# Empty edge slots: zeroed in DRAM ahead of the scatters, or masked in SBUF as they are read

## The chip, the cores and the metric

The kernel runs on one core of a Trainium2 chip. The metric is device time in microseconds of one execution; the median of three runs before the change is 2573.27 us (2565.25 to 2579.46). The profile is of one further execution, which took 2575.68 us; the span between its first and last instruction is 2573.9 us.

## The reference, cut to what matters

One launch computes a graph network layer and a mixing layer on the same normalised rows, adds both to the input, and then runs a mixture of experts. The change touches only the edges of the graph network: 50,000 edges between 3,125 nodes of 512 features (128 scalars and 128 vectors of three).

```python
ip1 = jnp.einsum('eum,eum->eu', p1[edge_dst], p1[edge_src]) / 3.0
s0 = jnp.concatenate([pd0, pd0, ip1], axis=-1)
...
w = ssp(edge_attr @ W_f1) @ W_f2 * (ssp(s0 @ W_s1) @ W_s2)
w1, w2, w3, w4 = jnp.split(w, 4, axis=-1)
x0e, x1e = split_irreps(x[edge_src])
sh0, sh1 = (edge_sh[:, 0], edge_sh[:, 1:4])
out0 = w1 * x0e * sh0[:, None] + w4 * (jnp.einsum('eum,em->eu', x1e, sh1) / jnp.sqrt(3.0))
out1 = w2[:, :, None] * x0e[:, :, None] * sh1[:, None, :] + w3[:, :, None] * x1e * sh0[:, None, None]
edge_feat = merge_irreps(out0, out1)
out = jax.ops.segment_sum(edge_feat, edge_dst, num_segments=old_x.shape[0])
```

Every term of an edge is multiplied by one of its four numbers `edge_sh`. An edge whose four numbers are zero adds nothing to any node.

## The kernel before, in words

**Where the edges go.** The edges are sorted by target on the chip. The 3,125 targets are cut into 25 groups of 125, each group into two halves of 63 and 62 (with one row shared). Each half has 8 tiles of 128 slots, 1,024 in all, for some 1,000 edges on average; edges beyond them go to shared late tiles. A tile of the first half and a tile of the second form a pair, two pairs form a quad of 512 slots. There are 200 fixed pairs and 8 late pairs that always run: 208 pairs, 104 quads. Further late pairs stand in a loop that runs only if they are needed; the inputs here do not need it.

**The record.** For each edge the first stage makes a record of 48 floats (192 bytes), of which 40 are used: the four numbers of `edge_sh`, the row numbers of source and target, the place of the target in its half, a zero, and 32 numbers of `edge_attr @ W_f1` after softplus. `recs` in DRAM has room for all slots, quad by quad; a quad is 128 x 4 x 48 floats, 98,304 bytes.

**The first stage** (up to 566 us). The edges come in 14 chunks of 28 tiles. For each chunk an attribute load on the SP queue (`edges_of`, L388) is followed by a product on PE (`spread`, L419), softplus on ACT and DVE, and the record is put together (`begin`, `joined`). Beside that, PE counts targets (L260) and ranks edges (`ranked`, L339 to L343), and DVE works out each edge's slot (`places`, L375). POOL then scatters a tile of records at a time into `recs` by an indirect DMA (`place`, L529), 391 in all. The order of the engines is written out by hand in `turns`; a scatter carries a dependence on a PE instruction, so that POOL gives way to PE. Every scatter waits for the DMAs in `cleared` (L183), which write zeros into some quads at the start; SP, ACT and POOL each issue DMAs, and all of these run on the same DMA engines. In the same stage run the layer norm, the mixing layer (`turn_x`, `keys_of`, L920 on) and the node parts of the graph network (L953 to L1032).

**The edge stage** (606 to 1650 us). Its order is the loop over `s` at L1352. For a quad, SP loads its records (`load`, L1104), DVE masks the empty slots (`clear`, L1109), DVE makes the one-hot rows of targets (`which`, L1142), PE turns them (`over`, L1150), POOL gathers the source and target rows (`fetch`, L1123 and L1127), DVE multiplies them (`products`), PE and ACT make the hidden layers, PE the weights (`weigh`, L1262 and L1263), ACT and DVE multiply those together (L1265, L1266), DVE makes the features (`feats`, L1280 and L1284), and PE sums them by target (`gather_up`, L1304). Each step runs some pairs ahead of the next.

**The mask.** An empty slot's record holds whatever lay in DRAM. `clear` combines all 40 used words bit by bit with a mask of all ones or zero, so an empty slot becomes a record of zeros: its rows are row 0, its four numbers 0. The table of masks is `real_slot`: `fixed_real` (L765) fills the fixed part from the number of edges that each half holds, `over_tiles` (L806) the late part.

Of the kernel before, what the change touches and what calls it, by code (L numbers as in the profile page):

```python
# [8 lines left out]
F32 = mybir.dt.float32  # L9
I32 = mybir.dt.int32  # L10
BF16 = mybir.dt.bfloat16
AF = mybir.ActivationFunctionType
ALU = mybir.AluOpType
# [4 lines left out]
P = 128  # L18
# [3 lines left out]
PER = 8  # L22
# [3 lines left out]
PR = 2  # L26
G = 4
REC = 48
# [8 lines left out]
NOV_MOST = 8  # L37
# [14 lines left out]
def gnn_mix_moe_kernel(ctx: ExitStack, tc: tile.TileContext, a: dict, out: bass.AP):  # L52
# [5 lines left out]
    nc = tc.nc  # L58
# [5 lines left out]
    NG = N // TG  # L64
    assert NG * TG == N and NG == NT and T * P >= EDGES > (T - CT) * P
    NU = 2 * NG
    NFIX = PER * NG
# [8 lines left out]
    def tn(t):  # L76
        return min(P, N - t * P)
# [7 lines left out]
    const = ctx.enter_context(tc.tile_pool(name="const", bufs=1))  # L85
# [16 lines left out]
    nc.vector.memset(half, 0.5)  # L102
    pairs_used = const.tile([P, 1], I32, name="pairs_used")
    pair_tile = const.tile([P, 2, NOV_MOST], I32, name="pair_tile")
    real_slot = const.tile([P, NFIX + NOV_MOST, PR], I32, name="real_slot")


    rows_d = dram.tile([N + 2, HID + 3 * MUL], F32, name="rows_d")
# [4 lines left out]
    recs = dram.tile([NQ * G * P, REC], F32, name="recs")  # L113
# [29 lines left out]
    with ExitStack() as c1:  # L143
# [4 lines left out]
        slot_no = srt.tile([P, NOV], I32, name="slot_no")  # L148
# [22 lines left out]
        for r in range(4):  # L171
# [5 lines left out]

        zero = tmp.tile([P, 3 * P], F32, name="zero")
        nc.vector.memset(zero, 0.0)
        by_quad = recs.rearrange("(q p i) f -> p q (i f)", p=P, i=G)  # L180
        per = PER // PR
        cleared = [
            nc.gpsimd.dma_start(by_quad[:, qs, :], zero[:, : G * REC].unsqueeze(1).to_broadcast([P, n, G * REC]))  # L183
            for qs, n in (
                (slice(per - 1, NFIX // PR, per), NG), (slice(NFIX // PR, (NFIX + NOV_MOST) // PR), NOV_MOST // PR),
            )
        ]
        for part in (slice(0, HID), slice(HID, HID + 3 * MUL)):
            nc.gpsimd.dma_start(rows_d[N:, part], zero[:2, : part.stop - part.start])
# [98 lines left out]
        held = srt.tile([P, NG, 2], F32, name="held")  # L288
# [177 lines left out]
        def load(name, shape, src, pool=w, tag=None):  # L466
            t_ = pool.tile(shape, F32, name=name, tag=tag or name)
            nc.scalar.dma_start(t_, src)
            return t_
# [292 lines left out]
        w1t = c4.enter_context(tc.tile_pool(name="w1t", bufs=1, reuse_waits="tile"))  # L762


        def fixed_real():  # L765

            is_real = w1t.tile([P, NG, PER, 2], F32, name="is_real")
            nc.vector.tensor_tensor(
                is_real, slot_no[:, :PER].unsqueeze(1).unsqueeze(3).to_broadcast([P, NG, PER, 2]),
                held.unsqueeze(2).to_broadcast([P, NG, PER, 2]), op=ALU.is_lt,  # L770
            )
            nc.vector.tensor_single_scalar(
                real_slot[:, :NFIX, :].rearrange("p s k -> p (s k)"),
                is_real.rearrange("p b j k -> p (b j k)"), -1.0, op=ALU.mult,
            )

        is_over = w1t.tile([P, NOV], F32, name="is_over")
        steps = w1t.tile([P, P], F32, name="steps")
        own_of = w1t.tile([P, 4], F32, name="own_of")
# [16 lines left out]
        def over_tiles(k):  # L796

            begun = w1t.tile([P, NOV], F32, name="begun", bufs=2)
            nc.vector.tensor_scalar(begun, pair_no, own_of[:, 2 + k : 3 + k], None, op0=ALU.is_ge)
            nc.vector.tensor_scalar(steps, ones, own_of[:, k : k + 1], None, op0=ALU.mult)  # L800
            ps = psum.tile([P, NOV], F32, name="ps_ov", tag="mm")
            nc.tensor.matmul(ps, steps[:NG, :], begun[:NG, :], start=True, stop=True)
            nc.vector.tensor_tensor(is_over, slot_no, ps, op=ALU.is_lt)
            late = w1t.tile([P, NOV], I32, name="late")
            nc.vector.tensor_single_scalar(late, is_over, -1.0, op=ALU.mult)
            nc.vector.tensor_copy(real_slot[:, NFIX:, k], late[:, :NOV_MOST])  # L806
            nc.sync.dma_start(late_real[k], late)
            ps = psum.tile([P, NOV], F32, name="ps_of", tag="mm")
            nc.tensor.matmul(ps, ones[:NG, :], begun[:NG, :], start=True, stop=True)
            late = w1t.tile([P, NOV], I32, name="late")  # L810
            nc.vector.tensor_scalar(late, ps, -1.0, None, op0=ALU.add)
            nc.vector.tensor_copy(pair_tile[:, k, :], late[:, :NOV_MOST])
            nc.sync.dma_start(late_tile[:, k, :], late[0:1, :])
# [81 lines left out]
        def lengths(c):  # L895
# [8 lines left out]
            0: [(sums_turned, 0)], 1: [(values, 0)], 2: [(values_turned, 0), (sums_turned, 1)],  # L904
            3: [(values_out, 0), (values, 1)], 4: [(values_turned, 1)], 5: [(values_out, 1)],
            6: [(through, w_nn[0][:, 1, :], w_nn[0][:, 0, :], w_o[0])], 7: [(through, w_nn[1][:, 1, :], w_nn[1][:, 0, :], w_o[1])],
            8: [(composed,)], 9: [(fixed_real,), (over_steps,)], 10: [(over_tiles, 0)], 11: [(over_tiles, 1)],
        }
        for c in range(NCH):
            pieces.setdefault(2 * c, []).append((lengths, c))  # L910
# [42 lines left out]
        for c in range(NCH):  # L953
# [23 lines left out]
            for t in tiles_of(c):  # L977
                n = tn(t)
# [16 lines left out]
                for o in range(2):  # L995
# [4 lines left out]
                    for i in range(2):  # L1000
                        b = 2 * o + i
# [76 lines left out]
    with ExitStack() as c2:  # L1078
# [27 lines left out]
        def clear(Q, real):  # L1106

            reci = Q.rec.bitcast(I32)[:, :, :USED]
            nc.vector.tensor_tensor(  # L1109
                reci, reci, real.rearrange("p s k -> p (s k)").unsqueeze(2).to_broadcast([P, G, USED]),  # L1110
                op=ALU.bitwise_and,
            )
# [211 lines left out]
        quads = [Quad() for _ in range(n_pairs // PR)]  # L1324
        pairs = [Pair(Q, j) for Q in quads for j in range(PR)]
        with tc.manual_schedule(engines=steady):
            LEAD = 9

            def due(at):

                q, r = divmod(at, PR)
                return [quads[q]] if r == 0 and 0 <= q < len(quads) else []

            def pair(at):

                return [pairs[at]] if 0 <= at < n_pairs else []

            def late_tiles(at):

                return [pair_tile[0:1, k, at - NFIX : at - NFIX + 1] for k in range(2)]  # L1340

            def kept(at):

                if not 0 <= at < n_pairs:
                    return
                R = pairs[at]
                if at >= NFIX:
                    keep_sums(late_tiles(at), R.ps)
                elif at % PER == PER - 1:
                    nc.scalar.copy(acc[:, at // PER, :], R.ps)  # L1350

            for s in range(-LEAD - 5, n_pairs + 1):  # L1352
                for Q in due(s + LEAD + 5):
                    q = quads.index(Q)
                    loaded = load(Q, recs[q * G * P : (q + 1) * G * P, :])
                    if q == 0:
                        for put in placed:
                            waits_for(loaded, put)
                for R in pair(s + LEAD + 3):
                    at = s + LEAD + 3  # L1360
                    if at >= NFIX and R.j == 1:
                        continue
                    if at >= NFIX:
                        R.own = targets([tile_of(nc.sync, v) for v in late_tiles(at)])
                    elif at % PER == 0:
                        R.own = targets([at // PER] * 2)
                    else:
                        R.own = pairs[at - 1].own
                kept(s - 1)
                for Q in due(s + 2):  # L1370
                    softplus2(Q)
                for R in pair(s + 7):
                    products(R)
                for Q in due(s + LEAD + 1):
                    q = quads.index(Q)
                    clear(Q, real_slot[:, PR * q : PR * (q + 1), :])
                    which(Q)
                for Q in due(s + LEAD):
                    over(Q)
                for R in pair(s + 1):  # L1380
                    weigh(R)
                for Q in due(s + 4):
                    hidden(Q)
                    hidden2(Q)
                for Q in due(s + 3):
                    softplus(Q, table)
                for R in pair(s + LEAD):
                    fetch(R.Q, R.j)
                for R in pair(s + 2):
                    scaled(R, 0)  # L1390
                for Q in due(s + 5):
                    turn(Q)
                    turn2(Q)
                for R in pair(s + 2):
                    scaled(R, 1)
                for R in pair(s):
                    if s >= NFIX or s % PER == 0:
                        sums = ps_a.tile([P, D], F32, name="ps_s")
                    R.ps = sums
                    gather_up(  # L1400
                        R, R.ps, s >= NFIX or s % PER == 0, s >= NFIX or s % PER == PER - 1
                    )
                for R in pair(s + 8):
                    own_rows(R)
                for R in pair(s + 1):
                    feats(R)
# [6 lines left out]
        with tc.If(some > NOV_MOST):  # L1413
            with tc.For_i(NOV_MOST // PR, (some + 1) // PR, 1) as i:
                Q = Quad()
# [34 lines left out]
    with ExitStack() as c3:  # L1450
# [18 lines left out]
        with tc.tile_pool(name="work3", bufs=2) as work:  # L1469
# [10 lines left out]
            with tc.manual_schedule(engines={mybir.EngineType.PE}):  # L1480
                oTs = {0: turned(0)}
                for t in range(NT):
                    n = P
# [101 lines left out]
            held = w.tile([P, NE, NT], F32, name="held")  # L1585
# [353 lines left out]
```

## Time and profile before

| | us |
|---|---|
| median of three runs | 2573.27 |
| lowest, highest | 2565.25, 2579.46 |
| the profiled execution | 2575.68 |
| its span | 2573.9 |
| first and last start of a scatter (L529) | 46.2, 564.2 |
| first and last start of a mask (L1109) | 568.6, 1641.4 |
| one mask, median | 0.317 |
| busy over the span: PE, DVE, ACT, POOL | 2347.7, 1634.8, 1254.0, 1529.1 |

A row of the timeline gives start and length in us, the engine, the line of the kernel, the operation with its tiles, and in square brackets how long the engine stood idle before it and what ended that. A name with a q (SPq, POOLq) is the engine's own issue of a DMA or a wait. A row of busy time by stretch gives for each engine its busy us and number of instructions, then the granted clock of TensorE (1.00 is full), the mean busy share of the 16 DMA engines, and GB/s. In the DMA view a queue's row gives packets, MB, and the time that its packets took as a share of 16 engines; q0 is POOL's queue, q1 SP's, q10 ACT's.

### The profile page before, as it was taken

What the parts mean: (1) busy time and instruction counts of PE and PEld (TensorE: products, weight loads), DVE (VectorE), ACT (ScalarE), POOL (GpSimd) and SP (SyncE); (2) the same over time, 40 slices, a digit from 0 to 9 for tenths busy, and PEclk for the clock granted to TensorE, in tenths of its full rate; (3) what the DMA queues carried; (4) which work ended last, traced back from release to release, by engine and by line L of the source; (5) the groups of instructions that cost most, each with busy time, mean ns of one, the idle gap of its engine ahead of it and who ended that gap; (6) DMA issues with size and microseconds to landing.
All of it is one profiled execution on the core that took longest, in us unless ns stands there. A gap on an engine that the chain in (4) does not pass through costs nothing. (4 is left out here: it accounts for less than half of the span.)

```text
span 2573.9 us, 46654 instructions
## 1 busy us (share of the span) xinstructions
PE 2347.7 (91%) x16977; PEld 1522.1 (59%) x16977; DVE 1634.8 (64%) x3130; ACT 1254.0 (49%) x3444; POOL 1529.1 (59%) x1488
## 2 busy tenths in 40 slices
PE   6888999408999999999999999984999999999998
PEld 4654456304444444444444444463888888888887
DVE  8887444207999999999999999976222222222222
ACT  2665512105777777777777777752222222222221
POOL 3777767776666666666666666413555555555552
PEclk7999999758999999999999999997999999999999
DMA  4665889528777777777777777545315325857454
GB/s 145 189 209 198 303 294 312 191 65 262 231 229 232 229 230 228 231 229 231 230 228 227 233 228 231 175 164 209 107 51 183 131 56 192 332 186 258 140 171 143
DMA packets 188092, 521.94 MB, mean 203 GB/s; under 512 B 55421, under 2 KB 84166, under 8 KB 177104
## 3 DMA queue, kind: packets, MB, share of 16 engines
q0 software_dynamic: 110224, 397.55, 48.2%
q1 hardware_dynamic: 71296, 115.05, 13.6%
q10 hardware_dynamic: 6336, 6.28, 0.8%
q8 instruction: 137, 2.24, 0.3%
q14 instruction: 99, 0.81, 0.1%
HBM read 586.07 MB, written 104.25 MB: 268 GB/s over the span
## 5 line engine op out<-in xcount | busy, mean ns | idle before, releaser
L1127 POOL DMA_INDIRECT gx<-rows_s,rec x416 | 445.5, 1071 | 326.5 <-DVE ft L1284 217.7
L1304 PE MATMUL ps_s<-ft,ones 128*64 128x256 f32 (+1 forms) x3328 | 493.8, 439 | 10.0 <-DVE acc L1318 9.9
L1250 ACT ACTIVATE ones<-one,rec 128x64 f32<-128x64 f32 x1664 | 429.5, 337 | 0.0
L1800 PE MATMUL ps_f<-h,we 128*128 128x128 f32 x3328 | 394.4, 277 | 1.2 <-DVE h L1815 1.2
L1813 ACT ACTIVATE h<-ps_f,bias 128x128 f32<-128x128 f32 x312 | 114.5, 368 | 575.2 <-PE ps_f L1800 558.7
L529 POOL DMA_INDIRECT recs<-again,at_i x335 | 326.3, 974 | 113.9 <-issue 78.9
L1800 PEld LDWEIGHTS ps_f<-h,we 128*128 128x128 f32 x3328 | 379.8, 192 | 3.1 <-DVE h L1815 1.6
L1284 DVE TENSOR_TENSOR ft<-wt,gx 128x768 f32<-128x768 f32 x416 | 378.3, 951 | 0.0
L1815 DVE TENSOR_SCALAR h<-ps_f,bias 128x128 f32<-128x128 f32 x312 | 108.6, 350 | 422.7 <-PE ps_f L1800 419.0
L1304 PEld LDWEIGHTS ps_s<-ft,ones 128*64 128x64 f32 x3328 | 222.2, 136 | 228.3 <-issue 148.5
L1720 POOL DMA_INDIRECT we<-w_rows,w_at x208 | 211.6, 1017 | 215.4 <-PE ps_y L1832 93.3
L1266 DVE TENSOR_TENSOR wt<-wt,wb 128x1024 f32<-128x1024 f32 x208 | 253.2, 1217 | 59.7 <-ACT wt L1265 59.2
L1123 POOL DMA_INDIRECT gd<-rows_d,rec x208 | 252.6, 1214 | 64.6 <-issue 64.3
L1265 ACT COPY wt<-wa 128x1024 f32<-128x1024 f32 x208 | 211.3, 1016 | 126.2 <-PE wb L1263 126.2
L1262 PE MATMUL wa<-w_f,hT 32*128 32x512 f32 x832 | 236.8, 640 | 0.0
L1263 PE MATMUL wb<-w_s,hT 32*128 32x512 f32 x832 | 235.8, 640 | 0.0
L1800 PEld LDWEIGHTS ps_f<-xt,we 128*128 128x128 f32 x1664 | 195.4, 193 | 25.5 <-issue 23.7
L1800 PE MATMUL ps_f<-xt,we 128*128 128x128 f32 x1664 | 195.8, 276 | 0.7 <-ACT xt L1748 0.7
L1832 PE MATMUL ps_y<-we,h 128*128 128x512 f32 x416 | 192.4, 605 | 0.1
L1182 PEld LDWEIGHTS ps_ip<-ident,prod 128*128 128x128 f32 x1248 | 136.6, 142 | 78.7 <-ACT oneT L1152 77.2
L1182 PE MATMUL ps_ip<-ident,prod 128*128 128x128 f32 x1248 | 161.6, 280 | 0.7 <-ACT oneT L1152 0.7
L1280 DVE TENSOR_TENSOR ft<-wt,gx 128x512 f32<-128x512 f32 x208 | 144.0, 692 | 7.1
(394 smaller groups left out, 3282.2 us busy)
## 6 DMA issues: line engine op xcount, KB each, us to landing
w_rows<-in_Wh SPq DMA_DIRECT2D x24, 1024.0 KB
rows_s<-r SPq DMA_DIRECT2D x24, 448.0 KB
rec<-recs SPq DMA_DIRECT2D x104, 96.0 KB
w_rows<-in_Wo SPq DMA_DIRECT2D x8, 1024.0 KB
lined<-rec SPq DMA_DIRECT2D x12, 672.0 KB
again<-lined POOLq DMA_DIRECT2D x12, 672.0 KB
gx<-rows_s,rec POOLq DMA_INDIRECT x416
xs<-acc POOLq DMA_DIRECT2D x25, 256.0 KB
```

What stands on the lines that cost most here:

```text
L529: put = nc.gpsimd.indirect_dma_start(out=recs[:, :], out_offset=bass.IndirectOffsetOnAxis(ap=at_i[:m, t : t + 1], axis=0), in_=again[c][:m ...
L1123: nc.gpsimd.indirect_dma_start(out=Q.gd[:, i - 2, :], out_offset=None, in_=rows_d[:, :], in_offset=bass.IndirectOffsetOnAxis(ap=reci[:, i, ...
L1127: nc.gpsimd.indirect_dma_start(out=Q.gx[:, i, :], out_offset=None, in_=rows_s[:, :], in_offset=bass.IndirectOffsetOnAxis(ap=reci[:, i, 4:5 ...
L1182: nc.tensor.matmul(ps[:, i, :], Q.prod[:, i, b * P : (b + 1) * P], ident, is_transpose=True, start=(b == 0), stop=(b == 2),)
L1250: nc.scalar.activation(R.ones[:, k, c, :], R.Q.one[:, i, :], AF.Copy, scale=R.Q.rec[:, i, c : c + 1])
L1262: nc.tensor.matmul(wa[:, k, :], Q.hT[r, 0, :], w_f2[r, :], start=True, stop=True)
L1263: nc.tensor.matmul(wb[:, k, :], Q.hT[q, 1, :], w_s2[q, :], start=True, stop=True)
L1266: nc.vector.tensor_mul(R.wt, R.wt, wb)
L1284: nc.vector.tensor_mul(R.ft[:, k, MUL : 7 * MUL].rearrange("p (b c u) -> p b c u", b=2, c=3), w[:, k, :, 1, :].unsqueeze(2).to_broadcast([ ...
L1304: nc.tensor.matmul(to, R.ones[:, k, m, :], what, start=(first and m == 0), stop=(last and m == 3), tile_position=(0, k * HT),)
L1720: nc.gpsimd.indirect_dma_start(out=dst, out_offset=None, in_=src, in_offset=bass.IndirectOffsetOnAxis(ap=at[:, j : j + 1], axis=0), bounds ...
L1800: nc.tensor.matmul(pss[f], ws[l][:, k, f * P : (f + 1) * P], h[:, k, :], start=(k == 0), stop=(k == 3))
```

## The change: zeros for all quads at the start, no masks

All 104 quads that always run are filled with zeros in DRAM, by four DMAs on POOL's queue, where two DMAs filled 29 of them before. The scatters wait for all four as they did for the two. The masking of the 104 quads in the edge stage is gone, with the table `real_slot` and the instructions that filled it. The one-hot of a quad and its gathers now wait for the record's load itself. In the loop for further late pairs the mask stays.

```diff
-    real_slot = const.tile([P, NFIX + NOV_MOST, PR], I32, name="real_slot")
...
         zero = tmp.tile([P, 3 * P], F32, name="zero")
         nc.vector.memset(zero, 0.0)
-        by_quad = recs.rearrange("(q p i) f -> p q (i f)", p=P, i=G)
-        per = PER // PR
+        n_zero = (NFIX + NOV_MOST) // PR * G * REC
+        step_z = zero.shape[1]
+        assert n_zero % (4 * step_z) == 0
+        by_part = recs[: n_zero * P // REC, :].rearrange("(p i) f -> p (i f)", p=P)
         cleared = [
-            nc.gpsimd.dma_start(by_quad[:, qs, :], zero[:, : G * REC].unsqueeze(1).to_broadcast([P, n, G * REC]))
-            for qs, n in (
-                (slice(per - 1, NFIX // PR, per), NG), (slice(NFIX // PR, (NFIX + NOV_MOST) // PR), NOV_MOST // PR),
-            )
+            nc.gpsimd.dma_start(
+                by_part[:, i * n_zero // 4 : (i + 1) * n_zero // 4].rearrange("p (a b) -> p a b", b=step_z),
+                zero.unsqueeze(1).to_broadcast([P, n_zero // 4 // step_z, step_z]),
+            )
+            for i in range(4)
         ]
...
-        def fixed_real():
-
-            is_real = w1t.tile([P, NG, PER, 2], F32, name="is_real")
-            nc.vector.tensor_tensor(
-                is_real, slot_no[:, :PER].unsqueeze(1).unsqueeze(3).to_broadcast([P, NG, PER, 2]),
-                held.unsqueeze(2).to_broadcast([P, NG, PER, 2]), op=ALU.is_lt,
-            )
-            nc.vector.tensor_single_scalar(
-                real_slot[:, :NFIX, :].rearrange("p s k -> p (s k)"),
-                is_real.rearrange("p b j k -> p (b j k)"), -1.0, op=ALU.mult,
-            )
-
...
-            nc.vector.tensor_copy(real_slot[:, NFIX:, k], late[:, :NOV_MOST])
...
-            8: [(composed,)], 9: [(fixed_real,), (over_steps,)], 10: [(over_tiles, 0)], 11: [(over_tiles, 1)],
+            8: [(composed,)], 9: [(over_steps,)], 10: [(over_tiles, 0)], 11: [(over_tiles, 1)],
...
                 for Q in due(s + LEAD + 1):
-                    q = quads.index(Q)
-                    clear(Q, real_slot[:, PR * q : PR * (q + 1), :])
                     which(Q)
```

A row of `by_part` is 19,968 floats (79,872 bytes) of one partition; each DMA writes a quarter of it, 13 pieces of 384 floats, on all 128 partitions.

## The prediction

> **What bounds the kernel now.** I read the busy time by stretch first: it says which stages there are and what is full in each.
>
> ```profile
> core 0: us, PE busy (x) PEld busy (x) DVE busy (x) ACT busy (x) POOL busy (x), PEclk, DMA share, GB/s
> 46.24:326.00 279.76, 239.59 (x993) 149.31 (x993) 209.63 (x744) 161.22 (x301) 212.96 (x221) 0.95 0.68 219
> 480.00:566.00 86.00, 0.91 (x3) 0.01 (x1) 2.48 (x12) 0.37 (x1) 64.87 (x68) 0.53 0.19 57
> 606.00:1650.00 1044.00, 1044.00 (x8783) 507.83 (x8782) 969.45 (x1285) 790.33 (x2397) 666.93 (x594) 1.00 0.75 230
> ```
>
> The change touches two stages. Up to 566 us the scatters of the edge records run one behind another on POOL (391 of them); from 480 us on everything else has finished and waits for them. From 606 to 1650 us the edge stage runs: PE is busy 1044.00 of 1044.00 us, VectorE (DVE) 969.45, which is 93%.
>
> Next the timeline of POOL around the scatters: when the first may start, and where the chain has slack.
>
> ```profile
> 46.24 1.04 POOL L529 DMA_INDIRECT recs<-rec,at_i  x1 [37.97 <-DVE at_i L375]
> 327.97 0.95 POOL L529 DMA_INDIRECT recs<-again,at_i  x1 [2.30 <-PE ps_p L987]
> 337.09 0.96 POOL L529 DMA_INDIRECT recs<-again,at_i  x1 [6.83 <-PE ps_nn L1002]
> 356.69 0.96 POOL L529 DMA_INDIRECT recs<-again,at_i  x1 [2.19 <-PE ps_p L987]
> 359.99 0.96 POOL L529 DMA_INDIRECT recs<-again,at_i  x1 [1.08 <-PE ps_nn L1002]
> ```
>
> The first scatter waits for its places from DVE (L375), not for the zeros that the kernel already writes. After that a scatter starts about every 1.27 us (0.96 and a gap of 0.30). Four waits for PE, above that ordinary gap, add up to 2.00 + 6.53 + 1.89 + 0.78 = 11.2 us. Here POOL is early: a POOL that starts up to 11.2 us late still ends on time, if PE is on time.
>
> Last, one period of the edge stage (a quad, 10.56 us), and a late pair behind it where PE had to wait:
>
> ```profile
> 801.42 1.22 DVE L1266 TENSOR_TENSOR wt<-wt,wb 128x1024 f32<-128x1024 f32 x1 [0.59 <-ACT wt L1265]
> 801.71 2.37 PE L1304 MATMUL ps_s<-ft,ones 128*64 128x512 f32 x16
> 803.28 1.82 DVE L1284 TENSOR_TENSOR ft<-wt,gx 128x768 f32<-128x768 f32 x2
> 806.09 0.32 DVE L1109 TENSOR_TENSOR rec<-rec,real_slot 128x160 int32<-128x160 int32 x1
> 806.34 2.37 PE L1304 MATMUL ps_s<-ft,ones 128*64 128x512 f32 x16
> 806.51 0.42 DVE L1142 TENSOR_TENSOR one<-lane,rec 128x256 f32<-128x256 f32 x1
> ...
> 1693.25 2.37 PE L1304 MATMUL ps_s<-ft,ones 128*64 128x512 f32 x16 [1.57 <-DVE acc L1318]
> ```
>
> The mask (L1109) is followed on DVE by the one-hot (L1142), the weights' product (L1266) and the features (L1284). The features of 803.28 end at 805.10 and PE sums them at 806.34, 1.2 us later; so PE does not wait for DVE. DVE itself waits 0.59 us per period for ACT, which waits for PE.
>
> **The change part by part.**
>
> *Masks taken out of the edge stage.* 104 instructions at L1109, median 317 ns: 104 x 0.317 = 33.0 us of DVE. Is any of it on the path? In each period PE follows itself without a gap: 2 x 2.37 (sums) + 1.53 (transposes) + some 2.4 (weights) + 1.3 (hidden layer) + 0.92 + 0.33 = 11.2 us, less the overlaps of neighbours, is the period. These lengths are PE's own and no hidden wait: the late pair at 1693.25 starts behind a wait and takes 2.37 us too. So the 33.0 us turn into DVE idle time; the work that hides them is PE's, with 1.2 us of margin. Without that cover they would cost up to 33.0 us.
>
> Here a rule of the Trainium skill speaks against me. "Perfetto Trace Analysis", section Identifying the Most-Contended Engine, says that matmul busy time is a poor measure, that weight-load busy time is the better one, and that the engine with the highest occupancy is the one to relieve. By that rule PE stands at 507.83/1044 = 49%, DVE at 93%, and the change gains nearly all of the 33.0 us. The row with the wait decides for me: a DVE that bounded the stage would not idle 0.59 us for ACT in every period with its features done 1.2 us ahead. I take 0, and keep -33 as the far end.
>
> *First quad.* Before, one-hot and gathers wait for the mask: the record lands at 568.56, mask until 568.89, one-hot, first gather at 569.68. Now the record alone counts: at least the mask's 0.33 us, at most the whole 1.1 us. I take -0.6, near the mask's own row.
>
> *Small DVE work.* L768 0.56 us, L772 0.36 us and two copies at 0.17 us, together 1.3 us, between 248 and 312 us. That stretch feeds PE and has DVE waits for PE and ACT of 2 to 4 us; 0, at most -1.3.
>
> *More zeros.* Before: 29 quads of 98,304 bytes, 2.85 MB. After: 104, 10.22 MB in four transfers on POOL's queue, and all four must land before the first scatter. POOL's issues were 1.76 and 0.82 us for 3,200 and 512 rows; by the same slope (0.35 ns a row on 0.64 us) four of 1,664 rows take 4.9 us, and POOL has nothing else to do until 46.24. What counts is the DMA engines. Two windows of the DMA view, 6 to 10 us and then 34 to 36 us (packets, MB, share of 16 engines):
>
> ```profile
> q0 software_dynamic: 273, 1.26, 98.9%
> q10 hardware_dynamic: 29, 0.01, 1.3%
> q1 hardware_dynamic: 43, 0.00, 0.8%
> ```
>
> ```profile
> q1 hardware_dynamic: 87, 0.19, 25.3%
> ```
>
> The zeros (q0) filled all engines: 1.26 MB in 4 us, 315 GB/s, 0.23 us for a packet of 4.6 KB. The second window holds only an edge-attribute load (L388), at 25% of 16: it runs on four engines, 32 packets of 3.5 KB on each, and 0.19 MB in 8.1 engine-us makes 0.15 us a packet.
>
> The zeros on the four shared engines: 10.22 MB / 16 = 0.64 MB each, 139 packets x 0.21 us (0.20 to 0.23) = 29 us. Beside them, from about 5 us on: two attribute loads at 32 x 0.15 = 4.8 us each, W_kT (1 MB) 3, three x tiles 2.3, a part of the third attribute load 3. Sum 5 + 29 + 18 = 52 us, with the ends 47 and 56. The places would be ready at 46.24 or a little later, so POOL starts some 2 to 9 us late. That lies within the 11.2 us of slack: 0 on the path.
>
> The rule for this is "DMA: Bandwidth & Descriptors", section Anatomy of one DMA: 2.0 us plus bytes at 436 GB/s. An estimate by it is 1.9 + 2.0 + 23.4 = 27 us, well ahead of the first scatter, and the new wait would never be seen. The rows show 315 GB/s even alone, and shared engines. I go by 52.
>
> *What the zeros delay.* This is the term that stays. PE's first hidden product (L419, at 21.80) waits for attribute load 0 in the middle of the counts (L260); behind the counts come DVE's sums (L267), the ranks, the places (L375). In program order PE and DVE stand still if that load is late; the x loads on SP also wait for it. In the profile the zeros end near 16 us, halfway through the load. With them going on, each of some 24 remaining packets per engine pays one more packet of 0.21 us at most, 5.0 us, against W_kT, which already took part of that time; PE has 0.8 us of slack at 28.6 to 29.36. So 0.5 to 4 us; I take 2.5. The stage until 326 us has PE and DVE 75 to 86% busy with waits on each other, and its loads are issued relative to it, so the shift carries through to the four waits above, to the last scatter, and to the edge stage.
>
> **Sum.** 2.5 - 0.6 + 0 + 0 = +1.9 us on the profiled execution's 2575.68 us (span 2573.9, 1.8 around it), 2577.6. The median of the runs is 2573.27, 2.4 below that execution; on it the forecast is 2575 us.
>
> **Rivals.**
>
> *DVE bounds the edge stage* (faster). For: 93% busy, and the rule above. Against: the 0.59 us, the 1.2 us of margin. Full effect 2573 - 33 + 2 = 2542 us; partly, up to 2558.
>
> *The zeros starve the other queues* (slower). For: in 6 to 10 us these moved 2.1%, though an attribute load had been issued at 5.59. If they wait until the zeros end near 36 us, load 0 lands at 36 + 4.8 = 41 instead of 21.8, PE and DVE shift by 18 us: 2573 + 18 - 1 = 2590. Against: from 10 to 16 us q0 held only 57.9% and the others 42%, so they do share once started. It decides (over 0.5%) if load 0 lands after about 36 us.
>
> *POOL alone is late.* The zeros' landing decides if it comes more than 11.2 + 13 us past 46.24, after 70 us. That needs 160 GB/s; nothing shows it. 2587.
>
> *Nothing is felt*: the zeros land early, the loads are not late. 2573 - 1 = 2572, in the likeliest case's own range.
>
> **How the numbers follow.** A difference under 0.5% (13 us) can't be told from no change here; the three runs spread over 14 us. The likeliest case, with "nothing is felt", 0.62: 2575, own range 2566 to 2584. DVE bound 0.14, of which 0.13 is beyond 0.5%. Starved queues 0.20 and late POOL 0.04, together 0.24 slower, of which 0.22 beyond the bound. So faster 0.13, same 0.65, slower 0.22. For the range I cut half of the fast case (below 2552) and the slowest tenth (above 2594).
>
> **What would show it.** Right: L1109 gone; the period still 10.56 us, DVE idle rising by 0.32 us in each; first scatter at 48 to 56 us, its wait ended by the zeros; L419 at 22 to 26 us; the four waits at L529 shorter by POOL's lateness; last scatter 1 to 4 us later than 564.21. Wrong: a period under 10.5 us (DVE was the bound), L419 after 30 us (starved queues), or a last scatter more than 10 us later.

## The result, and the profile after

| | before | after |
|---|---|---|
| median of 20 runs each, side by side, us | 2570.54 | 2581.49 |
| lowest, highest | 2564.97, 2579.46 | 2571.90, 2590.53 |
| ratio after / before, 95% interval | | 1.0041 [1.0030, 1.0052] |
| profiled execution, its span | 2575.68, 2573.9 | 2581.12, 2579.3 |
| first and last start of a scatter | 46.24, 564.21 | 51.23, 564.93 |
| first hidden product | 21.80 | 23.88 |
| period of the edge stage | 10.57 | 10.57 |
| last features' sum of the edge stage | 1700.28 | 1700.83 |
| DVE busy over the span | 1634.8 | 1601.2 |

The changed kernel is slower by 0.41%, which is 10.5 us (2570.54 x 0.0041). The forecast was 2575 us with a range of 2552 to 2594: the time lies inside it, and 0.41% lies inside the half per cent (the interval reaches 0.52%), but the forecast's own difference was 1.9 us, and 8.6 us of the measured one are not in its sum.

The busy time by stretch of the changed kernel comes first, with the same stretches as before.

```profile
46.24:326.00 279.76, 241.90 (x1017) 152.69 (x1017) 214.21 (x769) 161.69 (x302) 210.05 (x220) 0.96 0.68 220
480.00:566.00 86.00, 3.70 (x21) 2.05 (x19) 4.06 (x18) 1.10 (x3) 64.80 (x69) 0.55 0.22 69
606.00:1650.00 1044.00, 1044.00 (x8781) 507.49 (x8777) 937.34 (x1185) 789.97 (x2396) 684.62 (x594) 1.00 0.76 230
```

In the last row DVE has 32.1 us less to do (969.45 before), and PE is as full as it was.

One period of the edge stage, and the late pair, in the timeline of the changed kernel:

```profile
800.57 1.22 DVE L1255 TENSOR_TENSOR wt<-wt,wb 128x1024 f32<-128x1024 f32 x1 [1.02 <-ACT wt L1254]
800.87 2.37 PE L1293 MATMUL ps_s<-ft,ones 128*64 128x512 f32 x16
802.44 1.82 DVE L1273 TENSOR_TENSOR ft<-wt,gx 128x768 f32<-128x768 f32 x2
805.24 0.42 DVE L1131 TENSOR_TENSOR one<-lane,rec 128x256 f32<-128x256 f32 x1
805.50 2.37 PE L1293 MATMUL ps_s<-ft,ones 128*64 128x512 f32 x16
...
1692.41 2.37 PE L1293 MATMUL ps_s<-ft,ones 128*64 128x512 f32 x16 [1.57 <-DVE acc L1307]
```

The mask is gone, and DVE's wait for ACT ahead of the weights' product has grown from 0.59 to 1.02 us. The features end at 804.26 and are summed from 805.50, with the same 1.2 us between. PE follows itself as before.

The timeline of POOL has the first scatter and the waits for PE:

```profile
51.23 1.05 POOL L531 DMA_INDIRECT recs<-rec,at_i  x1 [40.02 <-DVE at_i L377]
335.85 0.96 POOL L531 DMA_INDIRECT recs<-again,at_i  x1 [4.52 <-PE ps_p L976]
354.42 0.96 POOL L531 DMA_INDIRECT recs<-again,at_i  x1 [1.20 <-PE ps_p L976]
357.47 0.96 POOL L531 DMA_INDIRECT recs<-again,at_i  x1 [0.83 <-PE ps_nn L991]
387.21 0.96 POOL L531 DMA_INDIRECT recs<-again,at_i  x1 [3.58 <-PE ps_nn L991]
```

The first scatter is 5.0 us late, and its places (L377, done at 50.95) end its wait, not the zeros: the last packet of the zeros ended at 44.96 us. So it is DVE that is late. Its timeline, before and after, shows where:

```profile
30.16 0.51 DVE L267 TENSOR_REDUCE sums<-ps_tot 56x50 f32<-56x350 f32 x1
36.73 0.68 DVE L555 BATCH_NORM_STATS2 bn<-x 128x6 f32<-128x512 f32 x1
45.77 0.19 DVE L375 TENSOR_TENSOR at_i<-at_i,side_i 128x28 int32<-128x28 int32 x1
```

```profile
31.51 0.51 DVE L269 TENSOR_REDUCE sums<-ps_tot 56x50 f32<-56x350 f32 x1
42.27 0.69 DVE L557 BATCH_NORM_STATS2 bn<-x 128x6 f32<-128x512 f32 x1 [4.11 <-DMA x<-in_x]
50.76 0.19 DVE L377 TENSOR_TENSOR at_i<-at_i,side_i 128x28 int32<-128x28 int32 x1
```

There are two delays. The sums of the counts are 1.35 us late, because PE's first hidden product (23.88 for 21.80) waited for attribute load 0. Then DVE stands for 4.11 us until the first tile of x has landed; before, it did not wait there. On SP's queue the load of x stands behind the second attribute load, and the trace's last packet of that load ends at 36.04 us, where it was 29.05. The places come out 4.99 us late.

The DMA view of the changed kernel, 6 to 10 us and then 34 to 36 us (packets, MB, share of 16 engines):

```profile
q0 software_dynamic: 342, 1.58, 101.0%
q10 hardware_dynamic: 25, 0.01, 1.1%
q1 hardware_dynamic: 48, 0.00, 0.9%
```

```profile
q0 software_dynamic: 157, 0.51, 63.3%
q1 hardware_dynamic: 84, 0.14, 18.1%
```

The zeros now move 1.58 MB in the first 4 us, 395 GB/s, where before they moved 315; a packet of 4.6 KB takes 0.187 us (64/342) instead of 0.23. The contiguous pieces are 1,536 bytes instead of 768, but the places in DRAM changed as well, and no run separates the two. At 34 to 36 us, where q1 had the engines to itself before (0.19 MB), it now moves 0.14.

One more delay is at the very end. The last two steps that the timeline shows, before and after:

```profile
2566.38 0.75 DVE L1769 SCALAR_TENSOR_TENSOR xg<-ps_y,share,xg 128x512 f32<-128x512 f32 x1 [2.54 <-PE ps_y L1832]
2568.89 1.01 POOL L1770 DMA_INDIRECT out<-xg,out_at  x1 [11.36 <-DVEq L1844]
```

```profile
2569.83 0.75 DVE L1756 SCALAR_TENSOR_TENSOR xg<-ps_y,share,xg 128x512 f32<-128x512 f32 x1 [2.54 <-PE ps_y L1819]
2570.86 1.01 POOL L1757 DMA_INDIRECT out<-xg,out_at  x1 [9.94 <-DVE xg L1756]
```

Between the end of the last product and the end of the span lie 6.8 us before (2567.13 to 2573.90) and 8.8 us after (2570.58 to 2579.35). In that stretch POOL runs two instructions which the page counts as neither busy nor waiting; I call them the end of its queue. The trace has (length in us):

```
                        before   after
INC_SWDGE_SEM           0.337    0.782
DRAIN                   0.727    2.523
```

They take 2.24 us more, of which 2.0 are left at the end. Nothing in the forecast's sum stands for this.

### The profile page after: what moved, and what is told of

Same layout as the page of the kernel before. It is cut to its first block, busy times and chain, and to the rows that moved or that the text cites. A ratio compares the mean times of both kernels' runs of the same rounds, so it can differ in the third digit from the quotient of the medians.

```text
span 2579.3 us, 46557 instructions
## 1 busy us (share of the span) xinstructions
PE 2348.4 (91%) x16977; PEld 1522.4 (59%) x16977; DVE 1601.2 (62%) x3022; ACT 1254.0 (49%) x3444; POOL 1546.8 (60%) x1490
## 3 DMA queue, kind: packets, MB, share of 16 engines
q1 hardware_dynamic: 71296, 115.05, 13.6%
q8 instruction: 137, 2.24, 0.4%
## 5 line engine op out<-in xcount | busy, mean ns | idle before, releaser
L1116 POOL DMA_INDIRECT gx<-rows_s,rec x416 | 452.0, 1087 | 308.0 <-DVE ft L1273 200.5
L1112 POOL DMA_INDIRECT gd<-rows_d,rec x208 | 264.5, 1271 | 64.6 <-issue 64.3
L1787 PEld LDWEIGHTS ps_f<-xt,we 128*128 128x128 f32 x1664 | 196.3, 194 | 25.5 <-issue 23.9
```

The costliest lines, as they stand in the source:

```text
L1112: nc.gpsimd.indirect_dma_start(out=Q.gd[:, i - 2, :], out_offset=None, in_=rows_d[:, :], in_offset=bass.IndirectOffsetOnAxis(ap=reci[:, i, ...
L1116: nc.gpsimd.indirect_dma_start(out=Q.gx[:, i, :], out_offset=None, in_=rows_s[:, :], in_offset=bass.IndirectOffsetOnAxis(ap=reci[:, i, 4:5 ...
L1787: nc.tensor.matmul(pss[f], ws[l][:, k, f * P : (f + 1) * P], h[:, k, :], start=(k == 0), stop=(k == 3))
```

## The experiments

The theory after the comparison: the zeros make the whole loss, through the late start of PE and DVE, which reaches the end by way of the scatters' waits for PE, and through the end of the queue; the masks cost and gain nothing. Rivals: POOL's late start counts in itself; or the removal of the masks has a price of its own; or the traffic slows the stage beyond its start.

The runs fell on four chips. On two (runs 5 to 8, and 12) the kernel before took 2578 and 2579 us with a period of 10.57 us, as in the result. On the other two (runs 1 to 4, and 9 to 11) it took 2789 and 2795 us: the profiles there show short stalls of all engines and mean periods of 11.1 to 11.5 us. I call these the stalling chips. Ratios are compared within a kind of chip.

### 1 and 5: the masks alone

The kernel before without masks and without `real_slot`, the zeros in 29 quads as they were. What it leaves out is the emptying of the slots in the other 75 quads, which keep what lay in DRAM.

```diff
-                    q = quads.index(Q)
-                    clear(Q, real_slot[:, PR * q : PR * (q + 1), :])
                     which(Q)
```

> The masks are gone, the zeros stay at the 29 quads of before (with these inputs only the last quad of each group has empty slots, so the output is the same). Theory A (the extra zeros cost the time, through a late first scatter; the masks are hidden behind PE): first scatter at 46.2 us, last at 564, period of the edge stage 10.57 us, time 0 to 1.5 us below before, ratio 0.999 to 1.000. Theory B (taking the masks out costs the time, later in the kernel): ratio 1.003 to 1.005, as with the whole change. Theory C (DVE bounds the edge stage): ratio 0.988.

> The first masks-off kernel again, on another chip: that run was on a chip where the kernel before took 2789 us, with stalls on all engines in every stage, so that it says little of a chip where it takes 2570 us. Theory A (masks hidden behind PE): ratio 0.999 to 1.000, period of the edge stage 10.57 us, first scatter 46.2 us. Theory B (taking the masks out costs later): 1.003 to 1.005. Theory C (DVE bounds): 0.988.

On the chip with the period of 10.57 us (run 5): 2580.82 us, ratio 1.0008 [0.9991, 1.0026], that is +2 us with an interval from -2 to +7. First scatter 46.56, end of the last product to the end 6.8 us, period 10.57. 32 us of DVE's work are gone and the time has not moved beyond that interval.

On the stalling chip (run 1): 2772.29 us, ratio 0.9936 [0.9914, 0.9958], that is 18 us gained. There the rows of busy time from 740 to 1640 us are, for the kernel with masks and all quads zeroed (run 2) and then for this one:

```profile
740.00:1640.00 900.00, 860.34 (x6954) 417.76 (x6950) 769.76 (x1016) 616.13 (x1896) 519.96 (x468) 0.99 0.69 210
```

```profile
740.00:1640.00 900.00, 875.23 (x7157) 429.15 (x7156) 765.78 (x965) 638.35 (x1951) 568.15 (x485) 1.00 0.71 217
```

PE is not full there (860 and 875 of 900 us), so it no longer covers DVE. Over 96 quads the mean period (from starts of the sums, L1304) is 11.43 us in run 2 and 11.36 in run 3, with masks, and 11.17, 11.13, 11.15 and 11.18 in the four kernels without them (runs 1, 4, 10 and 11): about 0.24 us less, most of one mask of 0.32. So in this kernel a mask costs nothing only as long as PE fills the stage.

### 2 and 6: the zeros alone

The kernel before with the four zero transfers of the change; the masks stay.

```diff
...
-            nc.gpsimd.dma_start(by_quad[:, qs, :], zero[:, : G * REC].unsqueeze(1).to_broadcast([P, n, G * REC]))
-            for qs, n in (
-                (slice(per - 1, NFIX // PR, per), NG), (slice(NFIX // PR, (NFIX + NOV_MOST) // PR), NOV_MOST // PR),
-            )
+            nc.gpsimd.dma_start(
+                by_part[:, i * n_zero // 4 : (i + 1) * n_zero // 4].rearrange("p (a b) -> p a b", b=step_z),
+                zero.unsqueeze(1).to_broadcast([P, n_zero // 4 // step_z, step_z]),
+            )
+            for i in range(4)
```

> All 104 quads are zeroed by four DMAs, the masks stay. Theory A: first scatter at 51 us, ratio 1.0035 to 1.005, all of what the change costs. Theory B: ratio 1.000.

> The zeros-only kernel again. Theory A (the zeros cost it all): first scatter at 51.2 us, ratio 1.0035 to 1.005. Theory B: 1.000.

Run 6: 2587.55 us, ratio 1.0037 [1.0025, 1.0050], +9.5 us (6.4 to 12.9). Run 2, on the stalling chip: 2799.01 us, 1.0035 [1.0013, 1.0057]. In run 6 the first hidden product is at 23.92, DVE waits 4.10 us for x, the first scatter is at 51.26, and the end takes 8.8 us, all as in the changed kernel. With run 5 this settles which part of the change costs: the zeros, as far as the intervals can tell all of it.

### 3 and 7: POOL alone late

The kernel before; POOL copies the first places and writes 12 rows of indices ahead of the first scatter. Zeros, DVE and PE are as before.

```diff
-        place(12)
+        late_i = tmp.tile([P, 256], I32, name="late_i")
+        nc.gpsimd.tensor_copy(late_i[:, :CT], at_i[:, :CT])
+        for _ in range(12):
+            late = nc.gpsimd.iota(late_i, pattern=[[1, 256]], base=0, channel_multiplier=0)
+        with tc.issue_after(late.ins):
+            place(12)
```

> Before, with POOL alone held up: a copy that needs the first places, and 12 iotas behind it, run ahead of the first scatter, which comes at about 50 to 51 us instead of 46.2. PE, DVE, ACT and the DMA queues are as before. If the four waits for PE between 326 and 360 us take up POOL's lateness, as the prediction has it: last scatter at 564 us, ratio 1.000. If POOL's chain sets the end in most executions (the waits for PE were long in the profiled one only): ratio 1.0015 to 1.002, 4 to 5 us.

> The kernel with POOL alone held up again; first scatter at 52.0 us, 5.7 us late, with DVE, PE and the DMA queues on time. If the waits for PE take up POOL's lateness: ratio 1.000. If POOL's chain sets the end in most executions: 1.0015 to 1.0025. If it is as slow as the whole change (1.004), the late start alone explains the change.

Run 7: 2577.28 us, ratio 0.9997 [0.9984, 1.0011]. The timeline of its POOL, at the first scatter and at the only long wait for PE left between 300 and 420 us:

```profile
51.68 1.06 POOL L529 DMA_INDIRECT recs<-rec,at_i  x1 [0.50 <-issue]
381.73 0.96 POOL L529 DMA_INDIRECT recs<-again,at_i  x1 [0.58 <-PE ps_nn L1007]
```

POOL is 5.4 us late and the waits of 6.83 and 2.30 us have shrunk to one of 0.58: POOL's lateness went into its slack, as the forecast had it, and the last scatter is not later (561.31). Run 3, on the stalling chip, gave 2793.87 us and 1.0035 [1.0014, 1.0055]. That contradicts run 7. In run 3 POOL stands idle for 172 us ahead of its last 335 scatters (104 us in run 7, 112 to 119 in the other profiles of the first kind of chip), so I use the stalling chips for no difference of a few us in this stage. Whether a late POOL is free there too stays open.

### 8: the kernel before, once more

> The kernel before, for a second trace: how much of its time between 326 and 566 us, and in the experts behind, varies from one execution to the next. If the slack of 11.2 us at the four waits belongs to that one execution, the waits here are shorter and the last scatter is before 564 us.

2583.83 us. Its first scatter is at 46.58 and its last at 571.13, 6.9 us later than in the other profile of the same kernel (564.21). A single profile cannot show where in this stage 5 us went; the near equality of last scatters before and after the change (564.21, 564.93) therefore says nothing.

### 4 and 10: x ahead of the second attribute load

The changed kernel, with the loads of the first three tiles of x moved on SP ahead of the second attribute load. Run 4 changed only that; in run 10 the statistics of the first x are also held behind the counts.

```diff
         edges_of(0)
+        xs_ = {}
+        for t in range(3):
+            xs_[t] = lnp.tile([P, D], F32, name="x")
+            nc.sync.dma_start(xs_[t], a["x"][t * P : (t + 1) * P, :])
         edges_of(1)
...
-            nc.vector.bn_stats(st[:n], x[:n])
+            if t == 0:
+                with tc.issue_after(counted_all.ins):
+                    nc.vector.bn_stats(st[:n], x[:n])
+            else:
+                nc.vector.bn_stats(st[:n], x[:n])
```

> The change, with the loads of the first three x tiles issued ahead of attribute load 1 on SP, so that they don't queue behind it. DVE's wait of 4.1 us for the x tile (start 42.27) should go. Theory A: first scatter at 47 to 49 us instead of 51.2, and with it 2 to 4 us of the loss: ratio to before 1.002 to 1.003, against 1.0041 of the change. If the first scatter's time doesn't matter: 1.004.

> The changed kernel with the loads of x of node tiles 0 to 2 issued on SP ahead of the second attribute load, and the statistics of x0 kept behind the counting on DVE, so that the order of every engine but SP is the changed kernel's. Theory A (of the 5 us, about 2 are the late first attribute load and about 3 the load of x0 that stood behind the second attribute load): DVE's wait for x0 falls from 4.1 us to under 1, first scatter at 47.5 to 49, ratio 1.0010 to 1.0025. Rival B (the x load is not on the path, or the second attribute load is then as late for the second tile): ratio 1.003 to 1.005, as the changed kernel's.

Run 4 missed its aim: the planner put the statistics of x ahead of the counts, DVE waited 21.81 us for x at 28.34, the first hidden product came at 42.92 and the first scatter at 68.10. It took 2789.01 us, ratio 1.0002 [0.9979, 1.0025].

Run 10: 2782.26 us, ratio 0.9966 [0.9945, 0.9987]. DVE's wait for x is gone (the statistics are at 38.12), but the first scatter is at 53.83, 2.6 us later than in the changed kernel. The timeline of PE shows what took its place:

```profile
43.48 0.77 PE L421 MATMUL ps_h<-w_f,ea 128*128 128x128 f32 x2 [10.47 <-DMA ea<-in_edge_attr]
```

PE now waits for the second attribute load, until 43.48. My expectation was wrong: the order of the two loads only chooses which of them is late. In neither order does SP's queue bring both by the time they are wanted while the zeros run. The ratio can't be set against the changed kernel's, which was not run on such a chip; it is near the product of runs 1 and 2 (0.9936 x 1.0035 = 0.9971), so nothing was gained or lost that these runs can tell.

### 9 and 12: DVE and PE late, without the zeros' traffic

The kernel before, with four memsets on DVE within the first places.

```diff
             nc.vector.tensor_reduce(slot, mine, AX.X, ALU.add)
-            nc.vector.tensor_copy(slot_i, slot)
+            if c == 0:
+                for _ in range(3):
+                    nc.vector.memset(mine, 0.0)
+                held_up = nc.vector.memset(mine[:, :12, :], 0.0)
+                with tc.issue_after(held_up.ins):
+                    nc.vector.tensor_copy(slot_i, slot)
+            else:
+                nc.vector.tensor_copy(slot_i, slot)
```

> The kernel before, its zeros and masks as they were, with four memsets of a spare tile on DVE (three of 128x1400, one of 128x600) between the reduction of the first slots and the rest of the first places: DVE, and TensorE behind it, start about 5 us late, with no extra transfer. Theory A (the late start of DVE and TensorE is what the zeros cost): first scatter at about 51, ratio 1.0020 to 1.0045. Rival B (the traffic itself slows the first stage beyond the late start, or the late start is absorbed in the slack at the scatter chain's waits as GpSimd's alone was): ratio 0.999 to 1.001.

> The kernel of the run before with four memsets on DVE once more, hoped for on a chip where the edge stage's period is 10.57 us, since the runs on stalling chips can't tell a late DVE from a late GpSimd (1.0033 and 1.0035). Theory A (the late start of DVE and TensorE is what the zeros cost): first scatter at 51 to 52, last scatter and end 3 to 10 us later than in the kernel before, ratio 1.0015 to 1.0040, most of the 1.0037 that the zeros alone gave. Rival B (the late start is absorbed as GpSimd's was, and the zeros' traffic costs elsewhere): ratio 0.999 to 1.001.

Run 12, with a period of 10.57 us: 2582.74 us, ratio 1.0019 [1.0005, 1.0032], +4.9 us (1.3 to 8.3). POOL's timeline:

```profile
50.88 1.04 POOL L536 DMA_INDIRECT recs<-rec,at_i  x1 [42.65 <-DVE at_i L382]
```

The first scatter is 4.6 us late and the end of the last product to the end of the kernel is 6.8 us, as before the change. A late POOL was absorbed; the same lateness, when DVE and PE share it, comes through: 4.6 us at the start, 4.9 (1.3 to 8.3) in the time. The intervals of runs 7 and 12 ([0.9984, 1.0011] and [1.0005, 1.0032]) overlap a little, and they are from two chips.

Run 12 is not quite as late as the zeros make it. PE's first product at L642 shows it, here for run 12 and then for run 6 (zeros alone), where the line has other numbers:

```profile
68.36 1.88 PE L649 MATMUL ps_kx<-xn,kf 128*128 128x512 f32 x4
```

```profile
70.00 1.88 PE L645 MATMUL ps_kx<-xn,kf 128*128 128x512 f32 x4
```

In the four profiles on these chips with the zeros of before and nothing held up on PE and DVE (the kernel before, runs 5, 7 and 8) it starts at 62.95 to 64.35 us, 63.5 on average, and in the changed kernel at 69.98. So PE is 4.9 us late here in run 12 and 6.5 us with the zeros, which is more than the 5.0 us of the first scatter.

Run 9, the same kernel on a stalling chip: 2807.06 us, 1.0033 [1.0004, 1.0063], which tells nothing beside run 3.

### 11: the zeros twice

The changed kernel, with its four zero transfers issued twice.

```diff
-            for i in range(4)
+            for i in (0, 1, 2, 3, 0, 1, 2, 3)
```

> The changed kernel with its four zero transfers issued twice, 20.4 MB for 10.2. Theory A (in the changed kernel the zeros land ahead of the first scatter's inputs; with twice as many they land last): zeros landed at 70 to 80 us, the first scatter starts there, ended by the zeros and not by DVE; that is 20 to 30 us beyond the changed kernel's, of which the slack at the four waits for TensorE takes about 11: ratio 1.008 to 1.013; the first hidden product at 24 to 26. Rival B (the cost follows the traffic over the first stage and not the moment of the first scatter): the first hidden product and the x loads are late in proportion, ratio 1.007 to 1.009. Rival C (GpSimd's lateness is absorbed wherever it comes from): ratio 1.003 to 1.005.

2812.00 us, ratio 1.0069 [1.0038, 1.0101], on the chip of run 10. The timeline of POOL has the fifth transfer, the seventh, and the first scatter:

```profile
14.55 1.15 POOL L184 DMA_DIRECT2D recs<-zero  x1 [4.64 <-DMA recs<-zero]
...
37.86 1.15 POOL L184 DMA_DIRECT2D recs<-zero  x1 [9.69 <-DMA recs<-zero]
...
84.60 1.05 POOL L531 DMA_INDIRECT recs<-rec,at_i  x1 [36.77 <-DVE at_i L374]
```

The wait of the first scatter is put down to L374, but the last of its places was written at 51.36; the last zero packet ended at 83.21, so it was the zeros. Now they do decide. The first hidden product (24.21), the wait for x (3.39 us) and the places (51.2) are where the changed kernel has them: the delay of PE and DVE does not grow with the bytes, since the loads that are late have landed by 42.7 us, about when the first set of zeros is through (the eighth transfer, issued only once the fourth has landed, starts at 45.61).

Beside run 10, the nearest kernel on this chip, the time is 29.7 us longer and the first scatter 30.8 us later. Of the 29.7, 3.8 are at the end: the last product to the end of the span takes 13.6 us here (2797.16 to 2810.81), and 9.8 in run 10. So 26 of 31 us came through, give or take a few. That is the forecast's rival of a late POOL, with a slack of some 5 us where the forecast read 11.2.

## Why the prediction was right, and where its sum was wrong

**Masks taken out of the edge stage**, taken as 0 of 33.0 us: right, and shown by run 5 (1.0008 [0.9991, 1.0026]). The rule of the Trainium skill that spoke against it ("Perfetto Trace Analysis", section Identifying the Most-Contended Engine) would have had DVE, at 93%, as the engine to relieve; here it gains nothing, and the row with DVE's wait for ACT was the better guide. On the stalling chip half of the 33.0 us are real (run 1, 18 us). The forecast named that case: without PE's cover the masks cost up to 33.0. It did not expect chips where the cover is thinner.

**First quad**, -0.6: right in size, but lost in the sum. From the last scatter to the first one-hot it is 4.71 to 4.76 us in the four profiles with the zeros and masks of before, 4.06 in the changed kernel, 4.33 without masks (run 5).

**Small DVE work**, 0: no run tells it from nothing; run 5 includes it.

**More zeros**, 0 on the path: right. POOL's lateness is absorbed (run 7), and there is a point from which it is not (run 11). The landing was estimated at 52 us (47 to 56) and came at 44.96, outside the ends. Two items were too large: at the 0.187 us measured, 139 packets make 26 us and not 29, and the third attribute load, priced at 3 us, had its packets only from 44.01 us on. (The window from 34 to 36 us held 12 packets of 2,048 bytes beside the attribute load, which it was said to hold alone; its 0.15 us a packet stands.) The estimate by the Trainium skill, "DMA: Bandwidth & Descriptors", section Anatomy of one DMA, was 27 us and further off. Its rate is not the reason: with the 395 GB/s measured here the same estimate is 30 us. It has no term for the loads beside the zeros. The mark "its wait ended by the zeros" was wrong for the same reason.

**What the zeros delay**, 2.5 us (0.5 to 4): this is the term that failed. The mechanism is right (run 12: lateness of PE and DVE comes through). Its size is 5.0 us at the first scatter and 6.5 us on PE at 70 us, above the upper end. I costed attribute load 0 alone (2.1 us measured at L421, 1.35 of it at the sums) and let "the x loads on SP also wait for it" stand as a remark without a price. It had one: DVE's 4.11 us for x0, behind the second attribute load.

**What the sum had not**: the end of POOL's queue, 2.0 us in the profile. From the end of the last product it is 6.7 to 7.0 us to the end of the span in all eight profiles with the zeros of before, 8.5 to 9.8 in the five with the new ones, and 13.6 with these twice.

With the first scatter's lateness the sum is 5.0 + 2.0 - 0.6 = 6.4 us, where 10.5 (7.7 to 13.4) was measured: it falls short of the interval. With PE's lateness at 70 us it is 6.5 + 2.0 - 0.6 = 7.9, just inside; for the zeros alone, 6.5 + 2.0 = 8.5 of 9.5 (6.4 to 12.9). That all of the 6.5 us reach the end is argued from run 12 and not shown by a run of its own. What is left, 1 to 3 us, these runs can't tell from nothing; whether the traffic costs anything beyond the late start stays open.

The rival "the zeros starve the other queues" had the right direction and too large a size: load 0 was ready for PE at 23.9 us, not 41.

Of the signs named for a right forecast, the first scatter (51.23 in 48 to 56) and the first hidden product (23.88 in 22 to 26) came. The last scatter came 0.7 us later and not 1 to 4, but run 8 shows that this sign is too noisy to count.

That the number held is in part luck. 2581.49 lies even in the likeliest case's own range (2566 to 2584), but near its upper end, and the median of the kernel before lay 2.7 us lower in the result than in the runs shown (2570.54 for 2573.27), so the change itself cost more than 2581.49 less 2573.27 shows. And 10.5 us stayed under the 13 us (0.5%) up to which the forecast spoke of no change; its +1.9 did not see that it would come so close.

## What to carry to other kernels

Whether a late engine costs anything is asked for each engine by itself: in this kernel, on the chips with the period of 10.57 us, 5.4 us on POOL cost nothing that could be measured (2.8 at most, run 7), and nearly the same on DVE and PE cost 4.9. When a bulk transfer is added at the start, list every load that will be waited for while it runs, by queue and in order, and give each a price; the first one in the list is not the only one. An engine at 93% beside one at 100% was worth nothing to relieve here, but only on chips on which the full engine really was full.

## What the runs showed of the hardware

**The end of POOL's queue had a price that grew with the zeros put into it.** POOL's last INC_SWDGE_SEM and DRAIN took 0.337 and 0.727 us with 3,712 pieces of zeros, 0.782 and 2.523 with 6,656, 1.717 and 6.362 with 13,312 (to within 0.01 us in all 14 profiles, on all chips). It is not simply a price per piece: the INC_SWDGE_SEM at 1656 us (the end of the edge stage's loop) took 2.142 us before the change and 0.453 after it. What it stands for, no run here shows.

**Zeros on POOL's queue and loads on SP's share the engines, and the loads pay.** With the zeros going on, attribute load 0 fed PE 2.1 us later (23.88 for 21.80), and the second attribute load's last packet ended 7.0 us later (36.04 for 29.05). In run 11, with the zeros twice, that load's last packet ended at 36.45 us, so the second set added next to nothing. Its transfers could not crowd in at the start: each writes where one of the first set wrote, and POOL waited for zeros to land before it issued each of them (4.64, 11.32, 9.69 and 6.60 us).

**The same kernel took 8% longer on two of the chips** (2789 and 2795 us for 2571 to 2579), with stalls on every engine: from 740 to 1640 us PE, DVE and ACT stand still together, for over 0.15 us at a time, for 11.9 us in run 2 and never in the kernel before. There the masks are worth 18 us instead of none. Why these chips stall, no run here shows.
